# Sixteen zero fills behind the first image's preparation, and three PSUM banks for the first image of the last layer

## The chip, the cores and the metric

The kernel runs on one core of a Trainium2 chip. The metric is the device time of one execution in microseconds (us), the median over several executions. Engines are named as in the profile: PE (TensorE, with PEld for its weight loads), DVE (VectorE), ACT (ScalarE), POOL (GpSimd) and SP (SyncE, which here only issues DMA transfers).

## What is computed

Four images of 64 x 64 positions and 128 channels pass through four layers. Each layer takes a group norm of its input, applies its own function and adds the result to the input:

```
x = x + ss2d(gn(x))                    # layer 0: selective scan in four directions
x = x + fourier_mlp(gn(x))             # layer 1: truncated Fourier mixing, then an MLP
x = x + codano(gn(x))                  # layer 2: attention and mixing in Fourier space
x = x + neighbourhood_attention(gn(x)) # layer 3: 7 x 7 window, 4 heads
```

For layer 3 the reference computes `q, k, v` from the normed image, scores every position against the 7 x 7 window around it (zero padded), adds a position bias, takes a softmax, multiplies with `v` and projects. In layer 0 the state of the scan is multiplied by a vector C at each step; the kernel does that product on PE with C laid out in a matrix that is zero off its diagonal blocks.

## The kernel before

The layers run one after another over all four images (`network`, line 1634). All intermediate images (x1, x2, x3) are in device memory. SBUF and PSUM tiles come from pools that are opened and closed like a stack: when a layer closes its pools, the next layer's pools take the same addresses in the order in which they are opened. The order of the instructions on PE, ACT, DVE and POOL is written out by hand inside each `manual_schedule` block; SP is in none of those sets, so the order of the transfers on SP's queue is the compiler's.

**Layer 0** (`layer0`, line 83). First come the weights (lines 102 to 154). Among them `zeros`, a tile of 128 x 516 zeros (258 KB), is set on DVE (line 136) and written 16 times (line 139) into the four scratch tensors W00, W01, W10 and W11 of four parts each; 16 x 258 KB are 4.1 MB. Later each unit of the scan overwrites only the diagonal cells of these tensors (line 320) and loads 256 KB of them as the C weights (line 506). Then the first image is prepared alone (`before(0, ...)`, run at line 350): group norm statistics of its eight parts (lines 163 to 172: load `xs`, transpose on PE, `bn_stats` on DVE), and for each of eight parts a load `xt`, a transpose, the normed `xn`, a projection `zp`, and a 3 x 3 convolution as 2 x 9 matmuls `cv`, whose results go to device memory by rows (`xr`) and by columns (`xw`). After that the 128 scan units run, each of which first loads its input `u` (line 297); the preparation of image b + 1 runs beside the scan of image b.

**Layer 1** (line 725) opens four SBUF pools, `l1big` (four tiles of 16,384 bytes per partition, 65,536 in all), `l1tmp`, `l1small` and `l1w`, and later `l2set`, above the weights of layer 2 in `l2w`, which stay.

**Layer 2** (line 1377) opens, above the same `l2w`, `l2big` (seven buffers of 16,384 bytes, 114,688 in all), `l2tmp` and `l2small`. The sum of their tiles is 67,328 bytes for `l2tmp` and some 14,100 for `l2small`. Two images run in turn. The last thing that an image does is to store `m`, one of the big tiles, to x3 (line 1373; in the profile all of layer 2's work has line 883, that of a helper that records it).

**Layer 3** (line 1404) opens `l3w` for its weights, the two padded `kp` images and a small tile `zero` (45,500 bytes together), fills the borders of `kp` on POOL (line 1432), writes `zero` to the borders of the padded v images in device memory (lines 1434 and 1436) and then opens `l3big` (x and xn, two buffers each, 65,536 bytes), `l3tmp` and `l3small`, and four PSUM pools [...]: `psS` with two buffers of two banks for the scores, `psT` with two of one bank, `psO` and `psM` with one bank each.

`front(b)` (line 1443) prepares image b in pieces:

- it loads x (four transfers of 512 KB);
- eight times: four transposes of x into a bank `pg`, `bn_stats` on DVE, a copy into `xn` on ACT;
- `group_scale` (line 64), and two operations on DVE that norm `xn`;
- eight times: a bank `pv` of four products (eight MATMUL records), on DVE the sum `vt` with the bias, and two stores of `vt` to the padded v image;
- eight times: a product `pk` (two MATMUL records), which ACT writes into `kp`.

All its banks are the single one of `psM` (tag "m"), which `queries` and `project` share. The sixteen loads V of a row of windows (line 1511) read the padded v image. For images 1 to 3 the pieces of `front` are called one at a time inside the loop over the 32 score units of the image before; for image 0 they run alone, ahead of that loop (line 1542).

Of the kernel before, what the change touches and what calls it, by code (L numbers as in the profile page):

```python
# [2 lines left out]

# [7 lines left out]
F32 = mybir.dt.float32  # L11
# [5 lines left out]
P = 128  # L17
# [5 lines left out]
CH = 512  # L23
NCH = NT // CH
K4 = 4
WD = 32 * 129 * 16
# [56 lines left out]
def layer0(sh, A, x_in, x_out, scr):  # L83
# [6 lines left out]
    tc, nc = sh.tc, sh.nc  # L90
    with ExitStack() as ctx:
        pool = lambda name, bufs, **kw: ctx.enter_context(tc.tile_pool(name=name, bufs=bufs, **kw))
        wp = pool("l0w", 1)
        tmp = pool("l0tmp", 2)
        small = pool("l0small", 2)
        ps = pool("l0ps", 1, space=PSUM)
# [33 lines left out]

        w_out = wp.tile([P, 2, P], F32, name="w_out")
        nc.sync.dma_start(w_out, A["out_proj"].rearrange("(s p) o -> p s o", p=P))


        zeros = wp.tile([P, WD // P], F32, name="zeros")
        nc.vector.memset(zeros, 0.0)
        for name in ("W00", "W01", "W10", "W11"):
            for g in range(4):
                nc.sync.dma_start(scr(name)[g].rearrange("(p f) -> p f", p=P), zeros)
        A_neg = wp.tile([P, K4, 2, NS], F32, name="A_neg")  # L140
        nc.sync.dma_start(A_neg, A["A_logs"].rearrange("(k s p) n -> p k s n", k=K4, s=2))
        nc.scalar.activation(A_neg, A_neg, AF.Exp)
# [201 lines left out]
        ring = [0]  # L344
# [4 lines left out]

        for _ in before(0, any_bank, lambda place, f, *a, slots=1, **kw: f(*a, **kw)):  # L350
            pass
        units = [(b, k, c) for b in range(NB) for k in (1, 3, 0, 2) for c in range(NCH)]
        per = len(units) // NB
        u, v = fetch(*units[0])
# [102 lines left out]
        with tc.manual_schedule(engines=order):  # L457
            for i, (b, k, c) in enumerate(units):
# [14 lines left out]
                for n in range(NS):  # L473
                    slot = NS * i + n
                    g, q = divmod(n, 4)
# [242 lines left out]
def load_image(nc, x, x_dram):  # L718
    for q in range(4):
        nc.sync.dma_start(  # L720
            x[:, 8 * q : 8 * q + 8, :], x_dram[1024 * q : 1024 * q + 1024, :].rearrange("(j p) d -> p j d", p=P)
        )
# [654 lines left out]
def layer2(sh, w, wp, x_in, x_out, scr, wt):  # L1377
    tc, nc = sh.tc, sh.nc
    with ExitStack() as ctx:
        pool = lambda name, bufs, **kw: ctx.enter_context(tc.tile_pool(name=name, bufs=bufs, **kw))  # L1380
        ps = pool("l2ps", 3, space=PSUM)
        for name, shape in (("XG", [64, 5, P]), ("BD", [P, P])):
            w[name] = [wp.tile(shape, F32, name=f"{name}{n}") for n in range(2)]
            for t in w[name]:
                nc.vector.memset(t, 0.0)
        for t in w["XG"]:
            nc.vector.memset(t[:, 4, 64:65], 1.0)
        pools = pool("l2big", 1), pool("l2tmp", 1), pool("l2small", 1), ps
        paced = copy(sh)
        paced.nc = Pace(nc)  # L1390
        engines = {mybir.EngineType.PE, mybir.EngineType.Activation, mybir.EngineType.DVE, mybir.EngineType.Pool}
        free = [0, 1]
        pairs = [[] for _ in range(NB // 2)]

        def image(b):
            n = free.pop(0)
            yield from layer2_image(paced, w, pools, x_in(b), x_out(b), (scr(n), scr(2 + n)), wt, n, pairs[b // 2])
            free.append(n)

        with tc.manual_schedule(engines=engines):  # L1400
            paced.nc.in_turn((image(b) for b in range(NB)), 2)


def layer3(sh, A, x_in, out, v_pads):
# [3 lines left out]
    tc, nc = sh.tc, sh.nc  # L1408
    tt = nc.vector.tensor_tensor
    with ExitStack() as ctx:  # L1410
        pool = lambda name, bufs, **kw: ctx.enter_context(tc.tile_pool(name=name, bufs=bufs, **kw))
        wp = pool("l3w", 1)
# [24 lines left out]
        big, tmp, small = pool("l3big", 2), pool("l3tmp", 2), pool("l3small", 4)  # L1437
        psS, psT = pool("l3psS", 2, space=PSUM), pool("l3psT", 2, space=PSUM)
        psO, psM = pool("l3psO", 1, space=PSUM), pool("l3psM", 1, space=PSUM)
# [2 lines left out]

        def front(b):

            x = big.tile([P, NJ, DM], F32, name="x3")
            load_image(nc, x, x_in(b))
            xn = big.tile([P, NT], F32, name="xn3")
            image[b] = x, xn
            yield
            st = small.tile([P, NCH, 6], F32, name="gn_st", bufs=2)  # L1450
            for c in range(NCH):
                pg = psM.tile([P, CH], F32, name="pg3", tag="m")
                for q in range(4):
                    nc.tensor.transpose(pg[:, q * P : (q + 1) * P], x[:, 4 * c + q, :], sh.ident)
                nc.vector.bn_stats(st[:, c, :], pg)
                nc.scalar.copy(xn[:, c * CH : (c + 1) * CH], pg)
                yield
            s_, o_ = sh.group_scale(st, psM, small, "m")
            yield
            for c in range(0, NT, NT // 2):  # L1460
                xc = xn[:, c : c + NT // 2]
                nc.vector.tensor_scalar(xc, xc, s_, o_, ALU.mult, ALU.add)
            yield
            for c in range(NCH):
                pv = psM.tile([P, 4, P], F32, name="pv3", tag="m")
                for q in range(4):
                    nc.tensor.matmul(
                        pv[:, q, :],
                        lhsT=xn[:, (4 * c + q) * P : (4 * c + q + 1) * P],
                        rhs=w["qkv"][:, 2 * P : 3 * P],  # L1470
                        start=True,
                        stop=True,
                    )
                vt = tmp.tile([P, 4, P], F32, name="vt")
                tt(vt, pv, w["v_b"].unsqueeze(1).to_broadcast([P, 4, P]), ALU.add)
                rows = v_pads[b % 2][3 + 8 * c : 11 + 8 * c, 3:67, :].rearrange("(q r) c d -> r c q d", r=2)
                for r in range(2):
                    nc.sync.dma_start(rows[r], vt[64 * r : 64 * r + 64])
                yield
            for c in range(NCH):  # L1480
                pk = psM.tile([P, CH], F32, name="pk3", tag="m")
                nc.tensor.matmul(
                    pk, lhsT=w["qkv"][:, P : 2 * P], rhs=xn[:, c * CH : (c + 1) * CH], start=True, stop=True
                )
                nc.scalar.activation(
                    kps[b % 2][:, 3 + 8 * c : 11 + 8 * c, 3:67],
                    pk.rearrange("p (h w) -> p h w", w=64),
                    AF.Identity,
                    bias=w["qkv_b"][:, 1:2],
                )  # L1490
                yield
# [49 lines left out]
        with tc.manual_schedule(engines=engines):  # L1541
            for _ in front(0):
                pass
            rows = {0: queries(0, 0)}
            for s in range(NU + 6):
                b, p = divmod(s, 32)
# [18 lines left out]
                if s < NU:  # L1565
                    q, V = rows[s // 4]
                    ps = psS.tile([P, 2, CH], F32, name="ps3")
# [52 lines left out]
                if p == 7 and b + 1 < NB and s < NU:  # L1620
                    pieces = front(b + 1)
# [213 lines left out]
```

## Time and profile before

| | before |
|---|---|
| median of 3 runs | 8299.07 us (8296.89 to 8299.89) |
| span of the profiled run | 8299.4 us |
| PE busy, share of the span | 6571.5 us, 79% |
| DVE busy | 6753.8 us, 81% |
| ACT busy | 6229.0 us, 75% |
| POOL busy | 5482.7 us, 66% |
| granted PE clock, mean | 0.946 |

By the timeline, the first image of layer 0 is prepared until about 195 us, the scan runs to about 6030 us, layer 1 to 6636, layer 2 to 7689, and layer 3 to the end; in layer 3 the first score product starts at 7777.44. No engine is busy for the whole of the kernel: shares of busy time are means over stages of different kinds, so what an edit is worth has to be read in its own stretch. The chain of work that ended last is the view for that. It follows each instruction back to the one that released it. In a chain line the first number is the start and the second the length.

### The profile page before, as it was taken

What the parts mean: (1) busy time and instruction counts of PE and PEld (TensorE: products, weight loads), DVE (VectorE), ACT (ScalarE), POOL (GpSimd) and SP (SyncE); (2) the same over time, 40 slices, a digit from 0 to 9 for tenths busy, and PEclk for the clock granted to TensorE, in tenths of its full rate; (3) what the DMA queues carried; (4) which work ended last, traced back from release to release, by engine and by line L of the source; (5) the groups of instructions that cost most, each with busy time, mean ns of one, the idle gap of its engine ahead of it and who ended that gap; (6) DMA issues with size and microseconds to landing.
All of it is one profiled execution on the core that took longest, in us unless ns stands there. A gap on an engine that the chain in (4) does not pass through costs nothing.

```text
span 8299.4 us, 140501 instructions
## 1 busy us (share of the span) xinstructions
PE 6571.5 (79%) x52976; PEld 4171.0 (50%) x52976; DVE 6753.8 (81%) x7948; ACT 6229.0 (75%) x10246; POOL 5482.7 (66%) x2502
## 2 busy tenths in 40 slices
PE   7788888778788877888877777787779878686689
PEld 3444454444445444444544444454467766464456
DVE  2889999998999999889999999999944545645578
ACT  3899999989899898989988999999822213315467
POOL 0889889988888898888889999999800011020233
PEclk9899999999999999999999999999989988788799
DMA  6445555445555544455555445455442041331332
GB/s 127 153 143 188 162 164 176 158 156 166 176 168 172 173 165 161 157 169 168 176 179 170 157 156 185 174 174 181 148 103 43 23 118 35 87 101 31 96 94 79
DMA packets 1281977, 1163.78 MB, mean 140 GB/s; under 512 B 637973, under 2 KB 1075825, under 8 KB 1214354
## 3 DMA queue, kind: packets, MB, share of 16 engines
q1 hardware_dynamic: 1279618, 1153.06, 44.0%
q8 instruction: 417, 6.83, 0.3%
q14 instruction: 262, 2.15, 0.1%
q10 hardware_dynamic: 1680, 1.74, 0.1%
HBM read 962.66 MB, written 189.74 MB: 139 GB/s over the span
## 4 chain that ended last, share of the span: by engine, by line
PE 21%; ACT 11%; DVE 11%; issue 3%; DMA 2%; POOL 2%; SPq 1%; DVEq 0%; ACTq 0%; POOLq 0%
DVE h L492 4%; ACT hT L389 4%; ACT dA L491 4%; PE pt L379 2%; PE po L695 1%; PE pf L690 1%; POOL dB L485 1%; PE pz L883 1%; PE pu L883 1%; PE pt L1518 1%; DVE in_st L883 1%; PE pb L883 1%; DVE m L883 1%; PE pa L883 1%; PE ps L1572 1%
## 5 line engine op out<-in xcount | busy, mean ns | idle before, releaser
L492 DVE TENSOR_TENSOR_SCAN h<-dA,state,dB 128x512 f32<-128x512 f32 x4096 | 4958.8, 1269 | 361.5 <-ACT dA L491 247.2
L485 POOL TENSOR_TENSOR dB<-du,Bb 128x1024 f32<-128x1024 f32 x2048 | 4817.0, 2385 | 550.7 <-DVE h L492 381.9
L379 PE MATMUL pt<-ident,h 128*128 128x128 f32 x16384 | 2249.0, 281 | 1014.9 <-ACT hT L389 1010.0
L379 PEld LDWEIGHTS pt<-ident,h 128*128 128x128 f32 x16384 | 1838.5, 143 | 2051.6 <-ACT hT L389 1806.4
L491 ACT ACTIVATE dA<-delta,A_neg 128x512 f32<-128x512 f32 x4096 | 2746.1, 690 | 163.8 <-DVE h L492 140.8
L389 ACT COPY hT<-pt 128x1024 f32<-128x1024 f32 x2048 | 2068.3, 1010 | 176.9 <-PE pt L379 163.4
L414 PE MATMUL yT<-hT,W 128*32 128x256 f32 x16384 | 1396.9, 414 | 2.7 <-DVE y L430 2.1
L883 POOL COPY XG<-Xs 64x9 f32<-64x9 f32 (+2 forms) x44 | 10.9, 292 | 1020.8 <-ACT Xs L883 1020.7
L414 PEld LDWEIGHTS yT<-hT,W 128*32 128x32 f32 x16384 | 454.4, 150 | 352.0 <-issue 336.9
L214 PE MATMUL cv<-xn,taps 128*128 128x512 f32 x1152 | 612.8, 632 | 0.0
L1556 POOL TENSOR_TENSOR S<-S,sm 128x784 f32<-128x784 f32 x128 | 191.1, 1493 | 403.1 <-DVE sm L1554 251.9
L325 PE MATMUL dp<-xd,w_dt 65*128 65x512 f32 x512 | 298.1, 665 | 103.9 <-ACT Ct L312 91.8
L334 POOL TENSOR_TENSOR du<-delta,u 128x1024 f32<-128x1024 f32 x128 | 305.1, 2383 | 67.6 <-DVE delta L331 67.6
L214 PEld LDWEIGHTS cv<-xn,taps 128*128 128x128 f32 x1152 | 183.4, 188 | 234.0 <-issue 232.6
L306 PE MATMUL xd_ps<-u,w_x 128*48 128x512 f32 x512 | 251.8, 615 | 40.9 <-DMA u<-l_xw 16.8
L1563 ACT ACTIVATE S<-S,mx 128x196 f32<-128x196 f32 x512 | 227.9, 448 | 33.0 <-DVE mx L1590 32.4
L691 ACT ACTIVATE h<-pf,b 128x512 f32<-128x512 f32 x128 | 88.0, 687 | 146.7 <-PE pf L690 146.7
L331 DVE SCALAR_TENSOR_TENSOR delta<-delta,dp 128x512 f32<-128x512 f32 x256 | 169.2, 661 | 25.7 <-ACT delta L329 25.7
L325 PEld LDWEIGHTS dp<-xd,w_dt 65*128 65x128 f32 x512 | 79.4, 195 | 219.5 <-ACT Ct L312 150.4
L1432 POOL MEMSET kp<- 128x210 f32 (+1 forms) x8 | 1.8, 286 | 275.0 <-DMA x<-m 275.0
L328 ACT ACTIVATE delta<-dp 128x512 f32<-128x512 f32 x256 | 152.4, 595 | 28.4 <-PE dp L325 23.8
L329 ACT ACTIVATE delta<-delta 128x512 f32<-128x512 f32 x256 | 162.3, 634 | 8.1
(335 smaller groups left out, 7183.8 us busy)
## 6 DMA issues: line engine op xcount, KB each, us to landing
Bb<-l_B SPq DMA_DIRECT2D x512, 1024.0 KB
W<-l_W SPq DMA_DIRECT2D x512, 256.0 KB
l_y<-y SPq DMA_DIRECT2D x128, 512.0 KB
u<-l_xw SPq DMA_DIRECT2D x64, 512.0 KB
y<-l_y SPq DMA_DIRECT2D x64, 512.0 KB
u<-l_xr SPq DMA_DIRECT2D x64, 512.0 KB
V<-l_v SPq DMA_DIRECT2D x512, 49.0 KB
wr<-wt SPq DMA_DIRECT2D x128, 136.0 KB
```

Of the source, the lines that this page charges most:

```text
L214: nc.tensor.matmul(pm, lhsT=taps[:, s, t, :], rhs=xn[:, dy : dy + 8, dx : dx + 64], start=(t == 0), stop=(t == 8),)
L306: nc.tensor.matmul(xd_ps, lhsT=w_x[:, s, k, :], rhs=u[:, s, :], start=(s == 0), stop=(s == 1))
L325: nc.tensor.matmul(dp, lhsT=w_dt[:, k, s * P : (s + 1) * P], rhs=xd, start=True, stop=True)
L334: nc.gpsimd.tensor_tensor(du, delta, u, ALU.mult)
L379: nc.tensor.transpose(pt[:, j, s, :], G["h"][:, s, t0 : t0 + 32, :].rearrange("p t n -> p (t n)"), sh.ident)
L389: return lambda: nc.scalar.copy(hT, pt.rearrange("p j s d -> p j (s d)"))
L414: nc.tensor.matmul(U["yT"][e][32 * jo : 32 * jo + 32, qo % 2, :], lhsT=U["Ws"][G["g"]][:, :, 4 * q + j], rhs=hT[:, j, :], start=((e, jo) n ...
L485: nc.gpsimd.tensor_tensor(dB, du, B_now[:, q : q + 1, :].to_broadcast([P, 2, CH]), ALU.mult)
L491: nc.scalar.activation(dA, delta[:, s, :], AF.Exp, scale=A_neg[:, k, s, n : n + 1])
L492: nc.vector.tensor_tensor_scan(h[:, s, :, q], dA, dB[:, s, :], state[:, s, n : n + 1], ALU.mult, ALU.add)
L883: r = f(*args, **kw)
L1563: nc.scalar.activation(Sn, Sn, AF.Exp, bias=U["mx"][:, n : n + 1], accum_out=sm[:, n : n + 1])
```

## The change

Three edits. In layer 0 the setting of `zeros` and its 16 stores move, in the program's text, from the weights to behind the preparation of the first image. In layer 2 the pools are opened in another order: `l2tmp`, `l2small`, `l2big` instead of `l2big`, `l2tmp`, `l2small`; their sizes stay. In layer 3 `front(0)` takes its banks in turn from `psM` and from the two buffers of `psS`, whose score tiles aren't in use yet; for the other images it still takes `psM`. The first is for the wait of the first image's loads behind the zeros, the second for what of layer 3 must wait for the end of layer 2, the third so that PE need not wait for the reader of the one bank.

```diff
+import itertools
...
-        zeros = wp.tile([P, WD // P], F32, name="zeros")
-        nc.vector.memset(zeros, 0.0)
-        for name in ("W00", "W01", "W10", "W11"):
-            for g in range(4):
-                nc.sync.dma_start(scr(name)[g].rearrange("(p f) -> p f", p=P), zeros)
         A_neg = wp.tile([P, K4, 2, NS], F32, name="A_neg")
...
         for _ in before(0, any_bank, lambda place, f, *a, slots=1, **kw: f(*a, **kw)):
             pass
+
+        zeros = wp.tile([P, WD // P], F32, name="zeros")
+        nc.vector.memset(zeros, 0.0)
+        for name in ("W00", "W01", "W10", "W11"):
+            for g in range(4):
+                nc.sync.dma_start(scr(name)[g].rearrange("(p f) -> p f", p=P), zeros)
...
-        pools = pool("l2big", 1), pool("l2tmp", 1), pool("l2small", 1), ps
+        tmp, small, big = pool("l2tmp", 1), pool("l2small", 1), pool("l2big", 1)
+        pools = big, tmp, small, ps
...
         def front(b):
 
+            ring = itertools.count()
+
+            def bank(name):
+                if b == 0 and next(ring) % 3:
+                    return psS.tile([P, 2, CH], F32, name="ps3")[:, 0, :]
+                return psM.tile([P, CH], F32, name=name, tag="m")
+
...
-                pg = psM.tile([P, CH], F32, name="pg3", tag="m")
+                pg = bank("pg3")
...
-                pv = psM.tile([P, 4, P], F32, name="pv3", tag="m")
+                pv = bank("pv3").rearrange("p (q d) -> p q d", q=4)
...
-                pk = psM.tile([P, CH], F32, name="pk3", tag="m")
+                pk = bank("pk3")
```

## The prediction

> **What bounds the kernel now.** I read the page first. No engine is full over the whole span; layer 0's scan keeps DVE near nine tenths up to slice 29, and none of the edits touches the scan's instructions. What they touch are three stretches in which the big engines wait: the first 38 us, the change from layer 1 to 2 at 6636 us, and the stretch from 7689 to 7777 us. In the page's row of granted clocks the last of them falls into the 38th of 40 slices, and the slices around it are the lowest of the span; page rows only point there.
>
> ```profile
> PEclk9899999999999999999999999999989988788799
> ```
>
> Then the timeline from 0 to 38 us. The columns are start, length, engine, line, operation.
>
> ```profile
> 3.33 0.40 SPq L132 DMA_DIRECT2D w_out<-in_out_proj  x1
> 4.99 9.98 SPq L139 DMA_DIRECT2D l_W<-zeros  x16
> 15.02 0.65 SPq L141 DMA_DIRECT2D A_neg<-in_A_logs  x1
> 24.93 3.68 PE L169 MATMUL gn_ps<-ident,xs 128*128 128x128 f32 x16 [24.93 <-DMA xs<-in_x]
> ```
>
> The zeros' issue takes SP 9.98 us, and the loads that PE waits for stand behind it: A_neg is issued at 15.02, the convolution taps and `xs` after that, and PE first works at 24.93. The windows of 2 us give a DMA share of about 1 from 6 to 30 us, at 337 to 383 GB/s while the zeros pass. So both the queue and the transfer engines are full with them.
>
> SP's own timeline at the end of the preparation shows how the compiler fills this queue:
>
> ```profile
> 195.28 5.62 SPq L165 DMA_DIRECT2D xs<-in_x  x3
> 202.44 0.88 SPq L297 DMA_DIRECT2D u<-l_xw  x2
> ```
>
> The three `xs` are loads for image 1, which the program asks for later than the fetch of `u`. They went ahead because `u` had to wait for the last `xw` store. Likewise x of image 1 in layer 3, asked for inside the loop, is issued with x of image 0 (line 720, x8 from 7699.87). Work that is ready is thus pulled into a free place of SP.
>
> Next, the chain of waits around the start of layer 3 (start, length, what):
>
> ```profile
> 7689.11 3.17 DMA x<-m
> 7692.36 0.35 SPq L1423
> ...
> 7699.87 4.23 DMA x<-x
> ...
> 7704.34 1.10 PE pg L1454 x4
> 7705.53 0.71 DVE gn_st L1455
> 7706.31 0.59 ACT xn L1456
> ...
> 7731.59 2.09 PE pv L1467 x8
> 7733.70 0.70 DVE vt L1475
> 7734.45 2.09 PE pv L1467 x8
> ...
> 7754.47 2.09 PE pk L1482 x2
> 7756.58 0.70 ACT kp L1485
> ```
>
> After the last store of `m` is issued (7689.11), nothing of layer 3 starts until it has landed (7692.36); then 14 small transfers take SP to 7699.87, the load of x takes 4.47 us to the first transposes, and from there each piece of the front is a strict sequence: product, reader, next product into the same bank. The steps repeat every 2.52 us for `pg`, and every 2.86 us for `pv` and `pk`. The view of waits names the releaser:
>
> ```profile
> POOL kp L1432 <- DMA x<-m: 275.0, 1, 275.0
> DVE zero L1429 <- DMA x<-m: 3.4, 1, 3.4
> ```
>
> In `l3w`, `qkv` comes first, the `kp` take bytes 4,700 to 43,900 and `zero` lies behind: they spread over three buffers of `l2big`, of which the last `m` is one. It can't lie under all three, yet all wait for its store. So a pool waits for the whole of the pools whose addresses it takes, not for single tiles. The windows (us, then busy us of PE, PEld, DVE, ACT, POOL, then PE clock, DMA share, GB/s) show the clock of this stretch:
>
> ```profile
> 6635.90:6651.70 15.80, 5.43 (x32) 4.85 (x32) 5.22 (x10) 0.00 (x0) 0.00 (x0) 0.63 0.96 258
> 7689.00:7704.30 15.30, 0.00 (x0) 0.00 (x0) 0.61 (x3) 0.00 (x0) 1.81 (x8) 0.50 0.64 181
> 7704.30:7728.70 24.40, 10.06 (x36) 6.73 (x36) 8.25 (x16) 4.94 (x9) 0.00 (x0) 0.50 0.46 138
> 7728.70:7751.60 22.90, 16.58 (x64) 14.26 (x64) 6.70 (x9) 0.00 (x0) 0.00 (x0) 0.50 0.36 94
> 7751.60:7777.40 25.80, 18.68 (x18) 4.51 (x18) 0.00 (x0) 6.33 (x10) 0.00 (x0) 0.50 0.25 70
> ```
>
> PE runs at 0.50 throughout, though it is busy three quarters of the last two. The first of the five lines is the same work at the start of layer 2, `pg` with three banks: from its first load (6639.10) to the end of the eighth `bn_stats` (6651.66) it took 12.56 us. It serves as a model below.
>
> [...] ACT's copy of `pg` starts after DVE's `bn_stats` has ended (7706.31 after 7706.24), so a bank is held for 2.5 us with or without the change. [...] the first convolution's weight loads are 0.85 us apart at 37.45 us and 0.43 from 42.7, about 5 us later, and a `pv` piece is 2.05 us at half clock where eight such matmuls (`pj`, 7801.60) take 1.06 in the loop.
>
> **The change, part by part.**
>
> *Zeros.* SP loses 16 issues ahead of A_neg. A_neg then follows `w_out` (3.33 + 0.40, so about 3.8) in place of 15.02: 11.2 us earlier. The transfers gain as much, 4.1 MB at some 360 GB/s being 11.4 us. The rest of the preparation is one chain from those loads, so it moves with them: 11 us. Where do the zeros go? They are ready from the first few us, so the compiler will pull them into the first free place of SP. Before, SP issues `xs` 1 to 4, `xt`, `xs` 5 to 8, with its free time after that (26.05 + 2.97 to 33.10, and 33.5 to 43.1). I take it that they go there: 16 x 0.62 = 10 us of issue in some 14 us of free queue, with transfer engines that nothing else needs until the first stores at 43 (share 0.30 from 40 to 60 us). They must be there by the first write of `Ct` (212.38), 170 us later. Cost nothing; what hides them is the convolution of the first image (PE busy 146 of 157 us). DVE's memset, 0.49 us, falls into its waits. If they go between the `xs`, the gain shrinks to nothing; if behind everything, they stand before `u` on the path and give the 11 us back.
>
> *Pool order, layer 1 to 2.* Before, `l2big` starts on `l1big` and waits for the last store of x out of it: 6635.96 to 6639.05. Now 67,328 + 14,100 = 81,400 bytes lie below `l2big`, more than the 65,536 of `l1big`, so it lies on `l1tmp` and later pools, whose last reader is DVE's addition ending at 6635.93. The load of xg goes right behind the issue of that store (0.5 us): 2.6 us gained. `l2tmp` now waits for the store, but its first tile of weight (`wr`) is used 170 us later.
>
> *Pool order, layer 2 to 3.* `l3w` (45,500 bytes) now lies inside `l2tmp`, whose last reader is PE's `pb` product, at 7623. So the 14 small transfers, POOL's memsets and DVE's `zero` (0.38 us) go into the tail of layer 2, where SP issues 12 transfers in 50 us. `l3big` still reaches into `l2big` (from 81,400 on, `l3big` ends at 111,000) and waits for the landing at 7692.36, but x is issued then and not at 7699.87: 7.5 us.
>
> *Banks, `pg`.* By layer 2's model the eighth statistics end at 7692.4 + 12.6 = 7705.0; ACT's copy (0.58) and a half clock at first bring `gn_gm` to about 7706.0, before 7724.6. That is 18.6 us, of which 11.1 are new.
>
> *Banks, `pv`.* The group scale is as before (4.15 us). Then PE (2.05 at half clock) no longer waits for DVE (0.69). But `vt` has two buffers: a piece holds one for DVE's 0.69, two issues of 0.62 and a landing of about 2.4 (chain: `DMA l_v<-vt`, 2.40 us), 4.3 us for two pieces, so 2.15 a piece; with a V load between here and there I take 2.3. Seven steps: 7 x (2.86 - 2.3) = 3.9 us. Bounds: 2.05 and 2.86, so 0 to 5.7.
>
> *Banks, `pk`.* Before, 25.9 us from the last `vt` to the first score. Now `pk` 1 to 3 follow the `vt` releases, the third ends 2.2 us after the last; then PE is never idle: two at 2.08, three at 1.1 with the clock up, `pq` 1.2, its ACT 0.8: 11.7 us. Gain 14.2; with the clock at half to the end 5 x 2.08 and 2.1, so 10.3.
>
> The score tiles' buffers in `psS` are last read by ACT's `kp`, done before the first score; this adds no wait. The sixteen V loads of a row, 0.73 us of issue each, take SP 12 us, four units 12.5 (`po` at 7790.05 and 7802.59); the first V are ready when the first two `vt` have landed, some 25 us ahead of the first score and 38 ahead of the first `po`: enough for 16 `vt` stores (10 us) and row one. From the first score on, the order is the old one, 36.7 us earlier.
>
> Sum: 11 + 2.6 + 7.5 + 11.1 + 3.9 + 14.2 = 50.3 us; 8299.1 - 50.3 = 8248.8, call it 8249.
>
> **Rivals.** (a) The zeros take the places between the `xs` loads, or stand before `u`: for it, SP's free time was read from a queue ordered without them; against it, `xs` 5 to 8 come earlier in the program. Start gains 0: 8260. (b) The stores become the bound in the front, SP (1.24 us of issue a piece, and V between) in place of the bank, with PE stopping and its clock at half: `pv` gains 0 and `pk` 10.3: 11 + 2.6 + 18.6 + 10.3 = 42.5, so 8257; with V late as well by the 7 us that a row's sixteen issues and their landing can hold up the first units, 8264. (c) Slower: the compiler orders SP anew over the scan as well. SP waits there behind single transfers (line 340 for `dB`, up to 10.9 us at once), and were Bb or W issued 0.5 us late for each of the 128 units, 64 us would be lost: 8313. Against it: none of the scan's instructions, buffers or hand-written orders changes, and a shift of all alike leaves their order alone.
>
> **How the numbers follow.** As worked out 0.70, (a) 0.11, (b) 0.13, (c) 0.03, and 0.03 for gains that cancel to within 0.2%. Likeliest 8249. The low end takes the better bounds: transfer backlog gone at the start (2 us more) and `pv` and `pk` at the full clock (7 us): 8240. The high end takes in (a) and (b): 8265. A gain of over 0.2% is 16.6 us, so all but (c) and the cancelling case are faster: 0.94, 0.03, 0.03.
>
> **What would show it.** First `gn_ps` at about 14 us; `l_W<-zeros` after the eighth `xs`; xg of layer 2 issued 0.5 us after the last x store; `qkv` and `zero` issued before 7650; x of layer 3 issued as the last `m` lands; `pg` about 1.1 us apart, `pv` about 2.3 with waits for `l_v<-vt`, `pk` from 2.1 down to 1.1. It is wrong if A_neg is still issued after 10 us, if `l3w` still waits for `m`, or if the first score starts more than 55 us after the last `m` has landed (85.1 before, 48.4 expected).

## The result and the profile after

The changed kernel takes 8253.87 us (median of 4 runs, 8243.57 to 8270.06) against 8299.48 us before (8296.89 to 8303.81): the ratio is 0.9946, 95% interval 0.9929 to 0.9964. Compared once more, beside kernels that make parts of the change, it took 8245.83 us (8240.00 to 8256.03, 5 runs) against 8307.71 us (27 runs): ratio 0.9932, interval 0.9920 to 0.9944. (The ratios here and below are those on record, with their intervals; they are not quotients of the two medians, which would be 0.9926 for this one.) The forecast of 8249 from 8299.1 is a ratio of 0.9940, which lies inside both intervals.

The row of granted clocks on the page of the profile after has a 7 in the 38th slice, as before: slices of 206 us are too wide to show a stretch of 45 us, and only the windows further down do:

```profile
PEclk9999999999999999999999999999989989698799
```

The start, in the timeline of the kernel after (start, length, engine, line, operation, and in brackets what ended the wait):

```profile
3.34 0.40 SPq L133 DMA_DIRECT2D w_out<-in_out_proj  x1
3.78 0.47 SPq L135 DMA_DIRECT2D A_neg<-in_A_logs  x1
...
13.24 3.35 PE L163 MATMUL gn_ps<-ident,xs 128*128 128x128 f32 x16 [13.24 <-DMA xs<-in_x]
...
17.08 2.66 SPq L352 DMA_DIRECT2D l_W<-zeros  x4
...
23.55 4.82 SPq L352 DMA_DIRECT2D l_W<-zeros  x7
```

A_neg is issued at 3.78 instead of 15.02, and PE first works at 13.24 instead of 24.93. The zeros stand behind the eighth `xs`, the first four in front of the second `xt` and the next seven behind it; of the remaining five one comes at 33.34 and four at 34.52. From SP's own timeline at the end of the preparation:

```profile
192.59 0.88 SPq L291 DMA_DIRECT2D u<-l_xw  x2
...
201.34 0.33 SPq L308 DMA_DIRECT2D l_B<-xd  x1
```

`u` is fetched 9.9 us earlier than before (192.59 against 202.44). But for one load of `xs`, 0.47 us, SP then has nothing to issue until 201.34, a hole of some 7 us that an experiment below will use.

Between layers 2 and 3 POOL's first memset of `kp` had waited 275.0 us for the last `m`. In the view of waits after, it waits for a product of layer 2:

```profile
POOL kp L1434 <- PE pb L884: 205.7, 1, 205.7
```

and SP's timeline has the 14 small transfers from 7618.29, 66 us before the last `m` is issued, and after that `m` at once the load of x:

```profile
7618.29 0.35 SPq L1425 DMA_DIRECT2D qkv<-in_qkv_w  x1
...
7687.33 9.91 SPq L721 DMA_DIRECT2D x<-x  x8
```

The chain of waits at layer 3's start (start, length, what):

```profile
7683.94 3.18 DMA x<-m
...
7687.33 3.91 DMA x<-x
...
7691.48 1.09 PE pg L1463 x4
7692.57 1.71 PE ps L1463 x8
...
7706.82 0.70 DVE vt L1484
7707.54 0.57 SPq L1487
...
7708.16 2.40 DMA l_v<-vt
...
7710.69 0.70 DVE vt L1484
```

x is issued as soon as the last `m` has landed. The first `pg` pieces (those in score tiles bear the name `ps`) follow each other without DVE or ACT between them. In the `pv` stretch the chain no longer has product, reader, product: it goes through the issue of the `vt` store, its landing (2.40 us) and the next `vt`, as the view of waits says in one line (us in total, times, longest):

```profile
DVE vt L1484 <- DMA l_v<-vt: 9.7, 6, 3.5
```

PE's timeline for `pk`, where two matmuls are one piece (the fourth line has two pieces):

```profile
7717.01 2.07 PE L1491 MATMUL ps<-xn,qkv 128*128 128x512 f32 x2
7719.87 2.07 PE L1491 MATMUL ps<-xn,qkv 128*128 128x512 f32 x2 [0.79 <-ACT kp L1494]
7721.74 1.86 PE L1491 MATMUL pk<-xn,qkv 128*128 128x512 f32 x2
7723.44 1.88 PE L1491 MATMUL ps<-xn,qkv 128*128 128x512 f32 x4
```

The pieces come down from 2.07 to 0.94 us with the fourth. The windows of these stretches (us, then busy us of PE, PEld, DVE, ACT, POOL, then PE clock, DMA share, GB/s) show the clock, 0.50 throughout before, now 0.64 to 0.87 once `pg` has begun:

```profile
7684.30:7691.40 7.10, 0.00 (x0) 0.00 (x0) 0.00 (x0) 0.00 (x0) 0.00 (x0) 0.50 0.62 183
7691.40:7703.20 11.80, 7.47 (x36) 6.38 (x36) 7.95 (x16) 4.96 (x9) 0.00 (x0) 0.64 0.96 290
7703.20:7721.30 18.10, 13.26 (x68) 9.89 (x68) 6.77 (x10) 0.70 (x1) 0.00 (x0) 0.78 0.40 102
7721.30:7729.60 8.30, 7.45 (x15) 3.06 (x15) 0.05 (x1) 5.67 (x9) 0.00 (x0) 0.87 0.39 106
```

In stages, each time read from the two profiles in the same way (us):

| stage | before | after | difference | forecast |
|---|---|---|---|---|
| start to the first scan operation `h` | 225.5 | 214.1 | -11.4 | -11 |
| first to last `h` of the scan | 5780.0 | 5783.6 | +3.7 | 0 |
| layer 1, first to last reader of `pf` | 475.4 | 480.8 | +5.4 | 0 |
| last addition of layer 1 (its start) to the issue of xg | 3.87 | 1.18 | -2.7 | -2.6 |
| issue of xg to the last issue of `m` | 1050.4 | 1050.1 | -0.3 | 0 |
| last `m` issued to first `pg` | 14.88 | 7.18 | -7.7 | -7.5 |
| first `pg` to `gn_gm` | 20.27 | 7.94 | -12.3 | -11.1 |
| `gn_gm` to first `pv` | 4.15 | 3.87 | -0.3 | 0 |
| first `pv` to the end of the last `vt` | 22.79 | 18.07 | -4.7 | -3.9 |
| last `vt` to first score | 25.88 | 8.27 | -17.6 | -14.2 |
| first score to last store of `out` | 519.1 | 519.5 | +0.4 | 0 |

They sum to -47.5, and the spans of the two profiles differ by 47.4. The stretches that the change touches gained 57.0 (with the 0.3 us in layer 2); the scan, layer 1 and the last loop, in which it touches nothing, gave 9.5 back. Two questions follow: is the decomposition right, that is, do the parts act alone and add up, and do the 9.5 us belong to the change?

### The profile page after: what moved, and what is told of

Same layout as the page of the kernel before. It is cut to its first block, busy times and chain, and to the rows that moved or that the text cites. A ratio compares the mean times of both kernels' runs of the same rounds, so it can differ in the third digit from the quotient of the medians.

```text
span 8252.0 us, 140499 instructions
## 1 busy us (share of the span) xinstructions
PE 6565.0 (80%) x52976; PEld 4175.2 (51%) x52976; DVE 6752.9 (82%) x7948; ACT 6242.8 (76%) x10246; POOL 5485.1 (66%) x2502
## 4 chain that ended last, share of the span: by engine, by line
PE 21%; ACT 11%; DVE 11%; issue 3%; POOL 2%; DMA 2%; SPq 1%; DVEq 0%; ACTq 0%; POOLq 0%
DVE h L493 5%; ACT hT L390 4%; ACT dA L492 4%; PE pt L380 1%; POOL dB L486 1%; PE pf L691 1%; PE po L696 1%; PE pz L884 1%; PE pt L1527 1%; PE pu L884 1%; DVE in_st L884 1%; PE pb L884 1%; DVE m L884 1%; PE ps L1581 1%; PE pa L884 1%
## 5 line engine op out<-in xcount | busy, mean ns | idle before, releaser
L884 POOL COPY XG<-Xs 64x9 f32<-64x9 f32 (+2 forms) x44 | 10.9, 294 | 1022.7 <-ACT Xs L884 1022.7
L1527 PE MATMUL pt<-ident,S 128*98 128x128 f32 x1024 | 164.8, 285 | 3.3 <-POOL S L1565 1.9
```

Of the source, the lines that this page charges most:

```text
L884: r = f(*args, **kw)
L1527: nc.tensor.transpose(pt[:, half, hp, :], U["S"][:, e, hp, 98 * half : 98 * half + 98], sh.ident)
```

## The experiments

**The three parts, each alone, and the whole once more.** First the zeros, in the kernel before:

```diff
-        zeros = wp.tile([P, WD // P], F32, name="zeros")
...
         for _ in before(0, any_bank, lambda place, f, *a, slots=1, **kw: f(*a, **kw)):
             pass
+        zeros = wp.tile([P, WD // P], F32, name="zeros")
...
```

> The kernel before with the zeros alone moved. Theory (the start gains 11 us and the zeros cost nothing where they go): first gn_ps at about 13.2 us, first scan operation h at about 214 instead of 225.5, everything after it shifted by that, so 8299.5 - 11 = 8288.5. Rival (the zeros, now beside the convolution, or the shifted start take time from the scan or from layer 1, which lost 3.7 and 5.5 us in the profile after): the same start, but 8297 to 8300, with the scan again about 5784 us from its first to its last h instead of 5780.

Measured: ratio 0.9986 (0.9978 to 0.9994), 8295.19 us against 8307.71; 0.0014 of 8299.5 is 11.6 us. First `gn_ps` at 12.89, first `h` at 212.1. The scan took 5782.7 us, layer 1 475.4. The start is as expected, and layer 1 is as in the kernel before. The scan lies nearer to the rival's 5784 than to 5780; whether the zeros have a part in that is taken up with all the profiles, in the last section.

Then the order of the pools alone:

```diff
-        pools = pool("l2big", 1), pool("l2tmp", 1), pool("l2small", 1), ps
+        tmp, small, big = pool("l2tmp", 1), pool("l2small", 1), pool("l2big", 1)
+        pools = big, tmp, small, ps
```

> The kernel before with the order of layer 2's pools alone. Theory: xg of layer 2 issued 0.5 us after the last x store (2.7 us gained), x of layer 3 issued as the last m lands (7.8 us gained between that landing and the first pg): 8299.5 - 10.5 = 8289. pg still 2.5 us apart, pv and pk 2.86. Rival (the new pool order makes layer 1 or 2 itself slower by its changed waits, where the profile after lost 5.5 us): 8294 to 8300, with layer 1 longer than the 635.2 us that it takes from the scan's end to its last addition in the kernel before.

Measured: ratio 0.9987 (0.9979 to 0.9995), 8296.14 us, so 10.8 us of 8299.5. From the last addition of layer 1 to xg 1.18 us, from the last `m` to the first `pg` 7.38; all that follows up to the first score is as in the kernel before to 0.1 us, and layer 1 takes 475.3. The rival falls: layer 1 is not longer. (The median of 8296.14 is in the range that it named, but that range was reckoned from 8299.5, and the kernel before took 8307.71 in this comparison.)

Then the banks alone:

```diff
+            ring = itertools.count()
+            def bank(name):
+                if b == 0 and next(ring) % 3:
...
-                pg = psM.tile([P, CH], F32, name="pg3", tag="m")
+                pg = bank("pg3")
...
```

> The kernel before with the three banks of layer 3's first image alone. By the steps of the prediction: pg 11.1 + pv 3.9 + pk 14.2 = 29.2, so 8270. By the lines of the profile after (first score 42.3 us after the last m landing against 85.1 before, less 7.8 for the pools): 35, so 8264.5. Rival (the banks gain only as x arrives early, or the clock comes up only because the whole front lies closer to layer 2's work): under 25, 8275 or more.

Measured: ratio 0.9960 (0.9948 to 0.9972), 8270.09 us, so 33.2 us of 8299.5 (23 to 43 by the interval). In the profile the way from the last `m` to the first score is 51.0 us instead of 88.0, 37.0 less; 7.36 us to `gn_gm`, 17.90 for `pv`, 7.20 from the last `vt` to the first score. The rival, that the banks need the pools' earlier start and gain less than 25 without it, falls by these 37.0.

And the changed kernel once more, without an edit:

> The changed kernel again, beside its three parts. Theory (the parts are independent and add up): 8299.5 - 11 - 10.5 - 35 = 8243 plus what the run itself varies by; the profile after lost 3.7 us in the scan and 5.5 us in layer 1 by chance, so this profile has the scan at about 5780 us from first to last h and layer 1 at about 629.6 us from its first pf to its last addition or less. Rival (these losses belong to the change): scan again 5783.7 and layer 1 again 5 us longer, 8253.

Measured: ratio 0.9932 (0.9920 to 0.9944), 8245.83 us. The three parts alone took 0.0014, 0.0013 and 0.0040 off, together 0.0067; the whole takes 0.0068 off. That these agree so closely is luck, since each part is only known to some 7 to 10 us; firmer is the way from the last `m` to the first score, which is 7.5 us shorter with the pools, 37.0 with the banks, and 42.7 and 44.6 in the two profiles with both. The parts add up. In this profile the scan took 5776.5 us and layer 1 475.1, so the 3.7 and 5.4 us of the first profile of the changed kernel did not come back; the last section shows what they hang on. (The last loop took 526.5 here, 7 us more than before; more on that at the end.)

**What the zeros' place is worth.** If they are free only because SP and the transfers have a hole during the first convolution, they must cost something elsewhere. Here they are made from the first `u`, so that they can't be issued ahead of it:

```diff
         u, v = fetch(*units[0])
+        zeros = wp.tile([P, WD // P], F32, name="zeros")
+        nc.vector.tensor_scalar(zeros[:, 0:512], u[:, 0, :], 0.0, None, ALU.mult)
+        nc.vector.tensor_scalar(zeros[:, 512:516], u[:, 1, 0:4], 0.0, None, ALU.mult)
...
```

> The changed kernel with the zeros made from the first u (u times 0), so that their 16 stores can only be issued behind the fetch of u. Theory (they are free only because SP and the transfer engines have a hole during the convolution): the start to u as in the changed kernel, then 16 x 0.62 = 10 us of issue in front of the first Ct store and W loads, and the first scan operation h 10 to 14 us later, at 224 to 228, so 8256 to 8260. Rival (the scan's start waits for other things, and the stores hide there too): h at 214 to 216 and 8246.

SP's timeline of this kernel:

```profile
191.88 0.88 SPq L291 DMA_DIRECT2D u<-l_xw  x2
...
196.60 10.11 SPq L356 DMA_DIRECT2D l_W<-zeros  x16
206.82 0.59 SPq L308 DMA_DIRECT2D l_B<-xd  x1
```

The zeros take SP 10.11 us, and the load of `l_B` follows them at once. From the fetch of `u` to `l_B` it is 14.9 us instead of 8.75, and to the first `h` 26.5 instead of 21.6 (at 218.4). So they cost 5 us there and not 10 to 14: SP was idle for 7 us in this place anyhow, and half of the issue disappears in that. Both expectations missed, the first by a factor of two; its direction holds. The single run's 8242.75 us shows nothing of it, since its scan happened to take 5774.8 us, 9 less than in the first profile of the changed kernel.

The zeros written twice, in the place where the change has them:

```diff
-        for name in ("W00", "W01", "W10", "W11"):
+        for name in ("W00", "W01", "W10", "W11") * 2:
```

> The changed kernel with the zeros written twice. Theory (the hole in the convolution is far larger than the zeros): first scan operation h still at 212 to 215, 8246. Rival (their transfers, now 8.2 MB beside the first stores of z, xr and xw, hold up the preparation): u and h later by up to 10 us.

SP's timeline of this kernel, where the second set trickles in between the stores until 68 us:

```profile
37.54 4.96 SPq L352 DMA_DIRECT2D l_W<-zeros  x8
...
64.70 3.29 SPq L352 DMA_DIRECT2D l_W<-zeros  x5
```

First `h` came at 217.2. But the first `gn_ps` was already late, at 16.42, by the landing of the first `xs`, ahead of all zeros; from there to the first `h` it is 200.7 us, as in the changed kernel (200.9 and 200.1). So even twice the zeros cost nothing beside the convolution. The run's 8260.79 us contains a scan of 5786.2 and a layer 1 of 480.9.

**How much of the front is banks, how much is clock.** By the prediction `pk` was the largest part, and about half of it clock. Here `pk` stays in one bank:

```diff
-                pk = bank("pk3")
+                pk = psM.tile([P, CH], F32, name="pk3", tag="m")
```

> The changed kernel with pk left in psM's one bank, pg and pv in three. Theory (by the prediction's steps pk is the largest part, 14.2 us, and half of that is the clock, which PE's waits for ACT keep at 0.50): 8 pk at 2.86 us, clock 0.50 through all of them; from the last vt to the first score 24 to 26 us instead of 8.3, so first score 59 to 62 us after the issue of the last m. Rival (the clock stays up from the pv pieces, or comes up in spite of the waits): pk at 1.8 us, and 50 to 53.

The windows of the `pv` and the `pk` stretch, and a piece of the chain in the latter:

```profile
7700.56:7718.41 17.85, 10.97 (x64) 10.11 (x64) 6.72 (x9) 0.00 (x0) 0.00 (x0) 0.69 0.40 104
7718.41:7744.29 25.88, 18.68 (x18) 4.53 (x19) 0.00 (x1) 6.36 (x10) 0.00 (x0) 0.50 0.28 78
```

```profile
7735.63 2.09 PE pk L1491 x2
...
7737.74 0.70 ACT kp L1494
...
7738.49 2.09 PE pk L1491 x2
```

The clock is 0.69 over the `pv` pieces, where DVE still waits for stores, and 0.50 over all of `pk`, whose pieces are 2.86 us apart (7738.49 after 7735.63), product and reader in turn. From the last `vt` to the first score 25.88 us, exactly as in the kernel before, and 62.6 from the last `m`. PE is busy for 18.68 of these 25.88 us, 72%, and that doesn't bring the clock up. The rival falls.

The reverse, `pk` in three banks and `pg` and `pv` in one:

```diff
-                pg = bank("pg3")
+                pg = psM.tile([P, CH], F32, name="pg3", tag="m")
...
-                pv = bank("pv3").rearrange("p (q d) -> p q d", q=4)
+                pv = psM.tile([P, 4, P], F32, name="pv3", tag="m")
```

> The changed kernel with pg and pv left in psM's one bank and pk in three. Theory (the parts add up): pg 20.3 us to gn_gm, pv 22.8 us to the last vt, as before, and pk as in the changed kernel or up to 2 us better, since no store of vt is left to hold it up: 12 us from the last vt to the first score with the clock coming up after two or three pk, so first score about 66 us after the issue of the last m (88 before, less 7.8 for the pools, less 14). Rival (pk gains only because the pv pieces ahead of it leave PE busy and the clock up): clock at 0.50 to the end, 17 us from the last vt to the first score, 71.

```profile
7711.55:7734.35 22.80, 16.59 (x64) 14.23 (x64) 6.64 (x9) 0.00 (x0) 0.00 (x0) 0.50 0.37 94
7734.35:7746.31 11.96, 11.04 (x19) 4.38 (x19) 0.00 (x0) 6.38 (x10) 0.00 (x0) 0.76 0.27 76
```

11.96 us from the last `vt` to the first score, 66.3 from the last `m`; the clock is 0.50 in `pv`, 0.76 on average in `pk`. So `pk`'s own banks are worth 13.9 us, and the 17.6 that the changed kernel shows there contain 3.7 that depend on `pv` having banks too: PE then runs ahead of the stalled `vt` and has the first `pk` behind it when the last `vt` ends.

**Is the third bank needed?** Every second piece, instead of two of three, goes to a score tile:

```diff
-                if b == 0 and next(ring) % 3:
+                if b == 0 and next(ring) % 2:
```

> The changed kernel with every second piece (not two of three) moved to a score tile, so that psM's bank comes round every second piece. Theory (what the banks buy is the bank's hold divided by the number of pieces until it comes round): pg 2.5 / 2 = 1.26 us apart instead of about 0.9, so 7.9 us from the first pg to gn_gm become about 11; pv (bound by vt) and pk (2.9 / 2 = 1.4, below PE's own 2.05 at half clock) no longer; first score about 47.5 us after the issue of the last m instead of 43.4 to 45.3. Rival (PE's own time or the landing of x is the bound in pg): 7.9 us as before, and 44.

PE's timeline of this kernel:

```profile
7685.89 1.09 PE L1463 MATMUL pg<-ident,x 128*128 128x128 f32 x4 [24.79 <-DMA x<-x]
7686.77 1.06 PE L1463 MATMUL ps<-ident,x 128*128 128x128 f32 x4
7688.51 1.12 PE L1463 MATMUL pg<-ident,x 128*128 128x128 f32 x4 [0.68 <-ACT xn L1465]
```

The two pieces in psM are 2.62 us apart with one other between, so 1.3 each (the next one comes at 7691.04, 2.53 later); `pg` to `gn_gm` takes 10.93 us instead of 7.94 and the first score comes 49.6 us after the last `m`, where 45.3 and 43.4 are the times of the two profiles of the changed kernel. The bank's hold is the bound, as expected. The remainder of 2 us, not expected, lies in `pk`, 9.77 us instead of 8.27 and 7.21: the second and third `pk` took 1.80 and 1.91 us, those behind them 1.02 or 1.13.

**The new bound in `pv`.** With banks for the products, the repeating gap in `pv` is DVE's wait for the store of `vt`, which has two buffers (9.7 us in six waits, by the view of waits above). With four:

```diff
-                vt = tmp.tile([P, 4, P], F32, name="vt")
+                vt = tmp.tile([P, 4, P], F32, name="vt", bufs=4)
```

> The changed kernel with four vt buffers instead of two, in layer 3. Theory (vt's store is what stops PE in the pv pieces, and these stops throw the clock back to 0.50 for the first pk): pv pieces at 2.05, 2.05 and then six at 1.06 us, pk at 1.02 without a fall of the clock, so first score 5.7 us earlier against the issue of the last m (45.3 and 43.4 us in the two profiles of the changed kernel, so about 38), the whole 8246 - 6 = 8240. Rival 1 (SP's issue of the stores, 0.62 us each, is the bound): pv stays at 1.3 to 2.2 a piece, gain 0 to 2. Rival 2 (all V loads now stand behind all stores and come too late): the front gains 5.7 but the loop from first score to last store is longer than the 519 to 526 us of the profiles so far.

PE's timeline in `pv` and the first `pk` (eight matmuls are one `pv`), and the view of waits:

```profile
7696.55 2.07 PE L1476 MATMUL ps<-qkv,xn 128*128 128x128 f32 x8 [2.13 <-DVE xn L1471]
7698.41 1.86 PE L1476 MATMUL pv<-qkv,xn 128*128 128x128 f32 x8
7700.11 1.95 PE L1476 MATMUL ps<-qkv,xn 128*128 128x128 f32 x16
7701.89 1.06 PE L1476 MATMUL pv<-qkv,xn 128*128 128x128 f32 x8
7702.78 1.95 PE L1476 MATMUL ps<-qkv,xn 128*128 128x128 f32 x16
```

```profile
DVE vt L1484 <- DMA l_v<-vt: 2.6, 3, 1.6
```

The first two pieces take 2.07 and 1.86 us; from 7700.11 on, 3.6 us after the first began, they take 1 us (two in 1.95) and stay there: `pv` takes 11.78 us instead of 18.06, then `pk` 7.21 (clock 0.85 and 1.00 in these two stretches). First score 37.9 us after the last `m`, as expected (38). Ratio 0.9910 (0.9894 to 0.9927), 8230.72 us against 8300.84. The front explains 5.5 to 7.4 us of this; the step from 0.9932, measured apart, to 0.9910 would be 18 us, and this profile also has the shortest scan of all (5774.0 us), with which the buffers have nothing to do. The loop behind it, 518.1 us, isn't longer, so the V loads, now behind all stores, don't come too late. The wait for `l_v<-vt` falls from 9.7 to 2.6 us.

But the four buffers changed a second thing: the compiler now issues all sixteen stores in one row, where it had put V loads of the first rows between them. So that row of stores was made with two buffers, by giving those V loads to another queue:

```diff
-                    nc.sync.dma_start(V[:, bx, half, :], v_pads[b % 2][r0 : r0 + 7, 8 * bx : 8 * bx + 14, :])
+                    (nc.gpsimd if b == 0 and by < 3 else nc.sync).dma_start(V[:, bx, half, :], v_pads[b % 2][r0 : r0 + 7, 8 * bx : 8 * bx + 14, :])
```

> The changed kernel with two vt buffers as it has them, but the V loads of image 0's first three rows issued by GpSimd, so that SP issues the sixteen vt stores in one row, as it does with four buffers. Theory (the two buffers alone hold pv: 0.69 for vt, 1.24 for the issue of its two stores, 2.4 for the landing, 4.3 us for two pieces): from the first pv to the last vt 17 to 18 us, as in the changed kernel (18.06). Rival (the V loads between the stores were the cause, and four buffers helped only because they moved them): 12 to 14 us. The last loop may become longer, since GpSimd now issues transfers beside its additions; that is not what is asked here.

SP's timeline of this kernel, the sixteen stores without anything between:

```profile
7716.39 17.50 SPq L1487 DMA_DIRECT2D l_v<-vt  x16
```

Still 19.07 us from the first `pv` to the last `vt`, and 46.0 from the last `m` to the first score. The buffers are the bound, and the V loads between the stores were not. (The last loop grew to 536.3 us, with GpSimd's issue of 9.3 us per row standing in front of its additions; the run as a whole took 8282.23.)

One step further: four `vt` buffers, and layer 3's pool for x waits for single tiles of what lay at its addresses, not for all of it:

```diff
-        big, tmp, small = pool("l3big", 2), pool("l3tmp", 2), pool("l3small", 4)
+        big, tmp, small = pool("l3big", 2, reuse_waits="tile"), pool("l3tmp", 2), pool("l3small", 4)
```

> The changed kernel with four vt buffers, and with layer 3's big pool waiting tile by tile for the addresses it takes, so that x no longer waits for the landing of the last m. Theory: x issued right behind the last m (3.3 us earlier), first score 3.3 us earlier than with the four buffers alone, about 35 us after the issue of the last m; 8237. Rival (the transfers of m and x share the same engines, so that x lands no earlier): as with four buffers alone, 8240.

Measured: x is issued right behind the last `m`, the first `pg` comes 5.21 us after it instead of 7.21, and the first score after 35.8 instead of 37.9. So 2 of the expected 3.3 us arrive, and the rival, that x lands no earlier, falls. By SP's timeline x is issued 2.95 us sooner after the last `m` (0.06 us instead of 3.01 with the four buffers alone), but from there to the first `pg` it takes 5.15 us instead of 4.20; why was not shown. Ratio 0.9921 (0.9907 to 0.9935), 8235.62 us: beside 0.9910 with the four buffers alone, the intervals overlap, and 2 us can't be told at this spread. The version with four buffers is the fastest measured of all; its interval and that of the changed kernel (0.9920 to 0.9944) overlap by 0.0007.

## Why the prediction was right, and where its steps were off

*Zeros.* Right in size (11.4 for 11, and 11.6 alone) and in reason. They went where the forecast put them, behind the eighth `xs`, and written twice they still cost nothing. (Sixteen times 128 x 516 x 4 bytes are 4.23 million bytes, so at the forecast's 360 GB/s the transfers take 11.7 us, not 11.4; the 11 stand.) Rival (a), the zeros between the `xs` or in front of `u`, didn't occur. Behind `u`, in front of the scan's first loads, they cost 5 us; the place ahead of `u`, for which the rival gave 11, was not tried.

*Pool order.* Right at both places: 2.7 for 2.6, 7.7 for 7.5, and as a part alone nothing else moved.

*`pg`.* Right; layer 2's stretch as a model gave 11.1, it was 12.3. The clock was 0.67 in the model's stretch (6639.10 to 6651.66 before) and 0.71 here, from the first `pg` to `gn_gm`, where it came up for the last pieces (in the timeline, `pg` at 7696.62 took 0.66 us, the first one 1.09).

*`pv`.* The bound was the one named, the two `vt` buffers; 2.3 us a piece was taken and it is 15.26 us between the ends of the first and the eighth `vt` (7706.09 and 7721.35), so 2.18 each. The clock, taken at half in that step, came up in the middle of it (0.78 on average in the window above); with four buffers the pieces come down to 1 us (two in 1.95).

*`pk`.* Mechanism right, size off: 17.6 for 14.2. The third `pk` ended 2.25 us after the last `vt` (7723.6 after 7721.35; forecast 2.2). The term that failed is the one after it, "two at 2.08, three at 1.1", 7.5 us: the five remaining ones took 4.3 us (7723.60 to 7727.89), because the full clock came at 7723.44 and not two pieces later (0.50 from 7719.87 to 7723.44, 1.00 from there to 7727.89). Two pieces at half clock was the author's estimate; PE had been without a pause from the second `pk` on (7719.87), and not only from the fourth. `pq` and its ACT, put at 2.0, took 1.7. The 13.9 us that `pk`'s banks give alone lie close to the 14.2, but on another way: there the first `pk` waits for the last `vt`, and the forecast had three of them near it already.

*The sum.* The steps gave 50.3, the touched stretches gained 57.0, and the profiled run was shortened by 47.4. So the agreement of 8249 with 8253.87 is in part luck, two errors that cancel: `pg`, `pv` and `pk` were together 5.4 too small, and the profile after lost 9.5 us in stretches that the change doesn't touch. That with 8245.83 is luck too, since the kernel before took 8307.71 beside it; the gain there is 56 us by the ratio, close to the 57.0. The 5.4 us of layer 1 hang on the moment at which the layer happens to begin, and the 3.7 of the scan go with the clock granted in it; both are worked out in the last section. Rival (c), a new order of SP over the scan, didn't occur: SP's instructions in the scan stand in the same order in both profiles, and no loss of its size (64 us) is there. (The longest wait of the kind that it names is 14.0 us in the kernel before, not 10.9.)

*Rival (b).* Half of it came true: the `vt` stores did become the bound in `pv`. But `pv` gained 4.7 us all the same and `pk` didn't suffer, since the buffers, held until the stores have landed (2.40 us in the chain), are the limit and not SP's issue; with four buffers the same sixteen stores are issued in 11.7 us.

## What to carry to other kernels

When a strict sequence of product and reader is opened with more banks, look at once for the next buffer in the ring: here the banks moved the bound to the two `vt` buffers, and doubling those brought another 6 us of front (first score 37.9 us after the last `m` instead of 43.4 and 45.3). The zeros, ready early and needed late, cost nothing in the stretch in which SP was idle (200.7 us from the first `gn_ps` to the first `h` with twice of them, 200.9 and 200.1 with them once); behind `u`, where SP would have waited 7 us anyhow, their 10.11 us of issue cost 5. So read the hole in the queue's own timeline. And where a change is worth half a per cent, compare stage by stage between two events that the change can't move; totals of single runs here differ by more than one part of the change (8243.57 to 8270.06 in four runs of the changed kernel).

## What the runs showed of the hardware

**The granted clock moves on one grid of time.** The trace keeps the clock as stretches with a start, a length and a value. In all fourteen profiles the value is 0.50 or 1.00 and nothing between, and every change lies on a grid of 3.413 us that runs through the whole execution (none is more than 0.02 us off it). Below, a step is one interval of 3.413 us and a border is where two of them meet. Means such as 0.70 or 0.87 above are mixes of the two. The first border comes 0.28 to 3.37 us behind the first instruction, at another place from profile to profile (1.75 before, 2.47 in the changed kernel). The next two lines are neighbouring steps of the grid at the start of layer 1 in the changed kernel (columns as above); PE has work throughout:

```profile
6143.05:6146.46 3.41, 3.41 (x6) 1.33 (x5) 0.00 (x0) 1.38 (x2) 0.00 (x0) 0.50 0.00 0
6146.46:6149.87 3.41, 3.41 (x21) 2.45 (x20) 0.00 (x0) 2.07 (x3) 0.00 (x0) 1.00 0.00 0
```

**Layer 1** comes in two lengths, 475 and 481 us, with the same matmuls. The windows of the whole stretch, first in the profile of the changed kernel, then in that of the same kernel run again:

```profile
6143.20:6624.00 480.80, 440.72 (x2417) 357.24 (x2417) 250.13 (x646) 135.28 (x234) 0.00 (x0) 0.93 0.15 35
```

```profile
6137.50:6612.60 475.10, 435.09 (x2416) 352.55 (x2416) 250.50 (x646) 134.75 (x233) 0.00 (x0) 0.94 0.15 35
```

DVE and ACT are the same within 1 us; PE needs 440.72 us instead of 435.09, at a clock of 0.93 instead of 0.94. Layer 1 took 475.1 to 476.1 us in ten of the fourteen profiles and 480.8 or 480.9 in four. The four all have the zeros moved, but so have seven of the ten, one of them the changed kernel itself. In these profiles the place on the grid at which the layer begins parts them: its first `pf` starts 2.29 to 2.39 us after a border in the four, and 2.77 to 3.28 us after one in the ten (6142.03 against a border at 6139.64, so 2.39, in the first profile of the changed kernel; 6135.49 against 6132.21, so 3.28, in the second). The four then spend 71.5 or 71.6 us of the layer at half clock, the ten 52.7 to 57.1. Between 2.39 and 2.77 us the two lengths part, so a shift of the layer by half a microsecond, from whatever lies upstream, can go with 5 us more or less. Whether the zeros' new place makes the long form likelier can't be told from three profiles without it.

**In layer 3** the other place is the group scale of images 1, 2 and 3, where PE pauses for 1.44 or 1.45 and then for 0.70 us, the same in every profile. The window from 52 to 60 us after the first score, with the scale of image 1, before, after, and with four `vt` buffers:

```profile
7829.44:7837.44 8.00, 5.86 (x116) 4.54 (x108) 6.30 (x15) 7.94 (x23) 2.99 (x2) 1.00 0.15 42
```

```profile
7781.62:7789.62 8.00, 5.85 (x68) 4.33 (x67) 5.27 (x14) 7.91 (x23) 2.99 (x2) 0.70 0.21 60
```

```profile
7767.54:7775.54 8.00, 5.86 (x93) 4.44 (x92) 6.34 (x15) 7.58 (x20) 2.46 (x3) 1.00 0.32 93
```

At a clock of 0.70 the next row of queries starts 19.7 us after the one before instead of 16.7. The fourteen profiles have 42 such rows. They take 16.7 us where no step falls to half clock (5 rows), 18.3 with one step at half (14 rows) and 19.5 to 19.8 with two (23 rows). Put in order of where the first matmul of the scale (`gn_gm`) starts on the grid, they do not mix: from 3.27 us after a border to 0.37 us after the next no step falls, from 0.63 to 2.23 us one, from 2.30 to 3.01 us two (in the first profile after, it starts at 2.61, 2.17 and 3.28 us, and the rows take 19.7, 18.3 and 16.7). So in these rows the same pause went with 0, 1.6 or about 3 us more, by its place on the grid. The three rows take 54.7 us together before and 54.7 in the first profile after, but 59.2 in the second: 4.5 of the 7 us by which its last loop was longer. The rest of these 7 us was not traced.

**In the scan**, where DVE is busier than PE (5401.5 against 4604.1 us of 5781.2 before), the length goes with the time at half clock as well. That time runs from 206.5 to 277.3 us over the fourteen profiles and the length from 5774.0 to 5790.7, with a correlation of 0.93 (230.2 and 5780.0 us before, 242.3 and 5783.6 in the first profile after); which of the two drives the other isn't shown. On average the scan took 5778.8 us in the three kernels with the zeros at the old place and 5781.3 in the eleven with them elsewhere, with 229 and 240 us at half clock. When the straight line through the fourteen is taken out, the two groups differ by 0.1 us, at a scatter of 1.7 us for a single profile. So the zeros do nothing to the scan that is seen beside the clock; whether they have a part in the clock's 11 us, within a range of 71 us, stays open.

**In `pk`**, with all of it in one bank, PE was busy for 18.68 of 25.88 us (72%), in pieces of 2.09 us with 0.77 us between, and the clock was 0.50 over all eight. In the changed kernel, where PE had no pause from 7719.87 on, it was 0.50 until 7723.44 and 1.00 from there to 7727.89.
